# Dense products of a 62-row chunk in two column halves on TensorE, in a four-layer graph network

## The chip, the cores and the metric

The kernel runs on one core of one Trainium2 chip. A core has five engines with their own instruction queues: TensorE (PE in the profile, its weight loads are PEld), VectorE (DVE), ScalarE (ACT), GpSimd (POOL) and SyncE (SP), which here only issues DMAs. ScalarE and GpSimd issue DMAs too, from the same queue as their arithmetic. SBUF holds the working data in up to 128 partitions, PSUM takes the results of TensorE. The metric is the device time of the core in microseconds.

## The reference, cut to what matters

There are 2,708 nodes with 512 features each and a dense 0/1 adjacency matrix `adj`. Each of four layers normalizes `x`, applies a ReLU, and adds the layer's output to `x`:

```python
# layer 0
out = (a.T @ h) @ weight;  out = out * clip(in_degree, 1)**-0.5;  x = x + relu(out)
# layer 1: each node's first 64 neighbours
x = x + leaky_relu(h @ W_line.T + b_line) + leaky_relu(mean_nb(h) @ W_nb.T + b_nb)
# layer 2: attention, 8 heads of 64
Wh = einsum('nd,hdo->hno', h, W);  x = x + elu(softmax(mask(leaky_relu(f1 + f2))) @ Wh)
# layer 3
combined = concat([h @ W_self + b_self, (mask @ h / deg) @ W_nb + b_nb])
x = x + relu(combined @ W_comb + b_comb)
```

Every layer thus has dense products of the 2,708 x 512 matrix `h` with 512 x 512 weights: one in layer 0, two in layer 1, one in layer 2, and two in layer 3 (there the kernel multiplies `W_comb` into the other two weights at the start, so that `self` and `nb` are one product each). Layers 0, 1 and 3 then aggregate over `adj`, layer 2 attends over it.

## The kernel before, in words

The nodes are cut into `NC` = 22 chunks of `R` = 126 rows; the last chunk, number 21, has `last_rows` = 62. The dense stage of a layer goes chunk by chunk: load `x` (`load_x`, line 277), normalize (`norm`, line 186), transpose four 128-column slices on TensorE and apply the ReLU on ScalarE (`relu_T`, line 208, giving `hT`), then multiply. `product` (line 182) is one dense product: four fp32 matmuls of a 126-column left side with 512 columns of weights, accumulated in one PSUM tile of 128 x 512.

What is aggregated is kept in SBUF as two fp32r numbers per value, a rounded one and the rest (`halves`, line 258): ScalarE copies the PSUM tile with rounding, VectorE subtracts the copy from the PSUM tile. An aggregation then runs one matmul with the rounded and one with the rest (`matmuls`, line 364). The last chunk has a form of its own, the tile `tail`. Its `x` was loaded twice, to partitions 0 to 61 and, from `TAIL` = 64, to partitions 64 to 125 (line 282), and so its product stands twice in PSUM, once in each half of the partitions. `tail` holds the rounded numbers in the lower half and the rests in the upper, and the aggregation takes both in a single matmul. In layer 2 the chunk is loaded once, and the product has 62 rows.

The places of the six products:

- `product0` (line 443), layer 0: dense stage and first aggregation step by step in turn, in one order of stages with lags (`staged`, line 625). Chunk 21 is the last product, and aggregation steps follow at once.
- `product1` (line 714), layer 1: `nb` and then `line` for each chunk. The first goes into `halves`; of the second, VectorE adds the bias (line 722) and applies the leaky ReLU (line 723), GpSimd adds it to `x` (line 726), and ScalarE's queue stores `x1` (line 727). `move` (line 95) cuts a store of 62 rows in two, 48 and 14 rows. The aggregation starts after chunk 21; VectorE makes its weights `kt` (`weight1`, line 739) in three buffers.
- `product2` (line 919), layer 2: ScalarE copies the result to `wh`, which is stored and multiplied with the attention vectors. Attention steps follow.
- `nb3` and `self3` (lines 1253 and 1258), layer 3: as in layer 1, with a bias add on VectorE (line 1263) and a store of `s3`. VectorE makes the aggregation's weights `kt3` (`weight3`, line 1294) after the check of the inputs (`judge`, line 1299) has begun.

Within an engine, work runs in the order of its queue, which the framework's scheduler lays down when the program is built. Order between engines is by semaphores. `load_weight` (line 170) fills one of two weight buffers, so a weight is loaded when the one before the last is no longer read: the weights `w2s` of layer 2 (line 737) take the buffer of layer 1's `wn`. Two reductions `wmax` over `w2s` (line 772) are VectorE work, and the scheduler has put them among the first `kt` of layer 1's aggregation. PSUM tiles come in turn from one pool of eight banks.

Of the kernel before, what the change touches and what calls it, by code (L numbers as in the profile page):

```python
# [8 lines left out]
F32 = mybir.dt.float32  # L9
# [6 lines left out]
ALU = mybir.AluOpType  # L16
# [6 lines left out]
R = 126  # L23

TAIL = 64
# [4 lines left out]
SLOPE1 = 0.01  # L30
# [14 lines left out]
def fast_layers(  # L45
# [36 lines left out]
    nc = tc.nc  # L82
    N, D = x_in.shape
    H, _, O = w2.shape
    NC = -(-N // R)
    NF = D // P
    O1 = O + 1

    last_rows = N - (NC - 1) * R
    assert last_rows <= TAIL and TAIL + last_rows <= R  # L90

    def rows(c):
        return min(R, N - c * R)

    def move(engine, dst, src):

        if dst.shape[0] == last_rows:
            cut = last_rows // 16 * 16
            engine.dma_start(dst[:cut], src[:cut])
            return engine.dma_start(dst[cut:], src[cut:])  # L100
        return engine.dma_start(dst, src)
# [68 lines left out]
    def load_weight(pool, src, name, tag=None, k=NF):  # L170
        w = pool.tile([P, k, src.shape[1]], F32, name=name, tag=tag or name)
        for i in range(k):
            nc.sync.dma_start(w[:, i], src[i * P : (i + 1) * P, :])
        return w

    def load_row(pool, src, name, tag=None):

        t = pool.tile([P, D], F32, name=name, tag=tag or name)
        nc.sync.dma_start(t, bass.AP(tensor=src.tensor, offset=src.offset, ap=[[0, P], [1, D]]))
        return t  # L180

    def product(po, lhsT, w, n):
        for f in range(NF):
            nc.tensor.matmul(po[:n], lhsT[:, f, :n], w[:, f, :], start=(f == 0), stop=(f == NF - 1))  # L184

    def norm(xc, n, scalar=False):

        st = small.tile([P, nc.vector.BN_STATS_DIM], F32, name="ln_st")
        nc.vector.bn_stats(st[:n], xc[:n])  # L189
        mv = small.tile([P, nc.vector.BN_AGGR_DIM], F32, name="ln_mv")  # L190
        nc.vector.bn_aggr(mv[:n], st[:n])  # L191
        rs = small.tile([P, 1], F32, name="ln_rs")
        nc.scalar.activation(rs[:n], mv[:n, 1:2], AF.Sqrt, bias=eps[:n], scale=1.0)  # L193
        nc.vector.reciprocal(rs[:n], rs[:n])
        hn = common.tile([P, D], F32, name="hn", tag="t", bufs=3)
        if scalar:
            shift = small.tile([P, 1], F32, name="ln_shift")
            nc.vector.tensor_scalar(
                shift[:n], mv[:n, 0:1], rs[:n], -1.0, op0=ALU.mult, op1=ALU.mult
            )  # L200
            nc.scalar.activation(hn[:n], xc[:n], AF.Relu, bias=shift[:n], scale=rs[:n])
            return hn
        nc.vector.tensor_scalar(
            hn[:n], xc[:n], mv[:n, 0:1], rs[:n], op0=ALU.subtract, op1=ALU.mult
        )
        return hn
# [30 lines left out]
    def dense(src, product_of, twice=True, more=(), scalar=False, rows_of=natural):  # L237

        kept = {}

        def size(c):
            return R if twice else rows(c)

        def load(c):
            kept[c] = load_x(src, c, twice=twice, rows_of=rows_of)

        def normalize(c):
            kept[c] = kept[c], norm(kept[c], size(c), scalar)

        def transpose(c):  # L250
            kept[c] = kept[c][0], relu_T(kept[c][1], size(c))

        def multiply(c):
            product_of(c, *kept.pop(c), size(c))

        return (0, load), (1, normalize), (2, transpose), (3, multiply), *more

    def halves(ring, po, c):

        if c < NC - 1:  # L260
            t = ring.tile([R, 2, D], F32R, name="halves")
        else:
            t = ring.tile([R, 1, D], F32R, name="tail", bufs=1)
        nc.scalar.copy(t[:, 0, :], po[:R])
        if c < NC - 1:
            nc.vector.tensor_tensor(t[:, 1, :], po[:R], t[:, 0, :].bitcast(F32), ALU.subtract)
        else:
            second = t[TAIL : TAIL + last_rows, 0, :]
            nc.vector.tensor_tensor(
                second, po[TAIL : TAIL + last_rows], second.bitcast(F32), ALU.subtract  # L270
            )
        return t


    loads = {}
# [135 lines left out]
    x1 = dram.tile([N, D], F32, name="x1")  # L411
    x2 = dram.tile([N, D], F32, name="x2")
    x3 = dram.tile([N, D], F32, name="x3")
    s3 = dram.tile([N, D], F32, name="s3")
    rT = dram.tile([H, NC * R], F32, name="rT")

    with ExitStack() as ring_ctx:
# [3 lines left out]
        stages1 = dense(  # L421
            x1,
            lambda *args: product1(*args),
            more=[
                (3, lambda c: save_last(c)),
# [6 lines left out]
        w0s = load_weight(weights, w0, "w0s", tag="w")  # L432
# [9 lines left out]

        def product0(c, xc, hT, n):
            po = ps.tile([P, D], F32, name="h0_ps", tag="ps")
            product(po, hT, w0s, n)
            h0[c] = halves(ring, po, c)

        with tc.tile_pool(name="l0", bufs=2) as wk:
# [173 lines left out]
            def first_dense(lag, fn):  # L622
# [3 lines left out]
                len(units),  # L626
                (0, load0),
                *[first_dense(lag, fn) for lag, fn in dense(x_in, product0, rows_of=paired)],
                (4, fenced(count0)),
                (5, fenced(sign0)),  # L630
# [12 lines left out]
        bl = load_row(wk, b_line1, "bl")  # L643
        bn = load_row(wk, b_nb1, "bn")
        wn, wl = l1_weights
# [68 lines left out]
        def product1(c, xc, hT, size):  # L714
            n = rows(c)
            pn = ps.tile([P, D], F32, name="nb_ps", tag="ps")
            product(pn, hT, wn, size)
            h1[c] = halves(ring, pn, c)
            po = ps.tile([P, D], F32, name="line_ps", tag="ps")
            product(po, hT, wl, size)  # L720
            y = common.tile([P, D], F32, name="y", tag="t", bufs=3)
            nc.vector.tensor_tensor(y[:n], po[:n], bl[:n], ALU.add)
            nc.vector.scalar_tensor_tensor(
                y[:n], y[:n], SLOPE1, y[:n], op0=ALU.mult, op1=ALU.max
            )
            nc.gpsimd.tensor_tensor(xc[:n], xc[:n], y[:n], ALU.add)
            move(nc.scalar, x1[c * R : c * R + n, :], xc[:n])

        def save_last(c):
            if c < len(groups[-1]):  # L730
# [4 lines left out]
        w2s = weights.tile([P, NF, H, O], F32, name="w2s", tag="w")  # L735
# [33 lines left out]
        def before1(c):  # L769
# [7 lines left out]
        stages2 = dense(  # L777
            x2,
            lambda *args: product2(*args),
            False,  # L780
            [(3, lambda c: save_last2(c)), (4, lambda c: sums2(c)), (6, lambda c: rows2(c))],
# [51 lines left out]
    row, weight, wh, whs, acc, sides, made, scaled = {}, {}, {}, {}, {}, {}, [], []  # L833
# [84 lines left out]

    def product2(c, xc, hT, n):
        po = ps.tile([P, D], F32, name="wh_ps", tag="ps")  # L920
        product(po, hT, w2s.rearrange("p f h o -> p f (h o)"), n)
        wh = pp.tile([R, D], F32, name="wh", bufs=3)
        nc.scalar.copy(wh[:n], po[:n])
        move(nc.sync, whd[c * R : c * R + n, :], wh[:n])
        for i in range(2):
            t = products[c, i] = pp.tile([R, H, O], F32, name="wh_a", bufs=4)
            eng = nc.gpsimd if i else nc.vector
            ins = eng.tensor_tensor(
                t[:n].rearrange("p h o -> p (h o)"), wh[:n], ar[i][:n], ALU.mult
            )  # L930
            if i == 0:
                firsts[c] = ins.ins
            else:
                nc.gpsimd.tensor_tensor(
                    t[:n, :, : O // 2], t[:n, :, : O // 2], t[:n, :, O // 2 :], ALU.add
                )
# [59 lines left out]
    kept3, l3_weights = {}, []  # L996
# [52 lines left out]
    def normalize3(c):  # L1049
        kept3[c] = kept3[c], norm(kept3[c], R)  # L1050
# [193 lines left out]
    with ExitStack() as stack:  # L1244
        ring = stack.enter_context(tc.tile_pool(name="ring3", bufs=NC - 1, reuse_waits="tile"))
        b3 = e3.tile([P, D], F32, name="b3", bufs=1)
# [4 lines left out]
        wself, wnb = l3_weights  # L1251

        def nb3(c):
            pn = ps.tile([P, D], F32, name="nb3_ps", tag="ps")
            product(pn, kept3[c][1], wnb, R)
            h3[c] = halves(ring, pn, c)

        def self3(c):
            n = rows(c)
            po = ps.tile([P, D], F32, name="self_ps", tag="ps")  # L1260
            product(po, kept3.pop(c)[1], wself, R)
            y = common.tile([P, D], F32, name="y", tag="t", bufs=3)
            ins = nc.vector.tensor_tensor(y[:n], po[:n], b3[:n], ALU.add)
            move(nc.scalar, s3[c * R : c * R + n, :], y[:n])
            return ins.ins

        def do(fn, c):
# [8 lines left out]
        for c in range(NC):  # L1276
            nb3(c)
            if c:
                do(transpose3, c + 1)
            do(turn3, c + 3)  # L1280
            do(normalize3, c + 2)
            do(save3, c + 2)
            do(elu3, c + 3)
            do(load3, c + 5)
            final = self3(c)
            if c == 0:
                transpose3(1)
# [691 lines left out]
```

## Time and profile before

| | |
|---|---|
| device time, median of 3 runs | 1822.22 us (1820.46 to 1822.46) |
| profiled execution, own time | 1820.7 us |
| its span, first to last instruction | 1818.8 us |
| mean granted TensorE clock | 0.996 |
| busy: TensorE, VectorE, ScalarE, GpSimd | 1781.6, 1307.9, 798.0, 245.3 us |
| last chunk's product in layer 0 | starts 162.46 us |
| last chunk's products in layer 1 | start 534.39 (record) us, aggregation from 541.40 us |
| last chunk's product in layer 2 | starts 850.11 us |
| last chunk's products in layer 3 | start 1581.47 us, aggregation from 1589.73 us |

The profile is one execution on the chip. Times inside it count from the start of its span. A group of instructions has a line of the kernel, an engine, an operation and shapes; the busy time of a group counts overlapping instructions once, while the mean is that of a single one, so a busy time below count times mean says that instructions overlapped. An fp32 matmul appears as two records. An arrow in brackets names what ended the idle time before an instruction. "The chain" is the work followed back from the last instruction, at each step to what released it.

### The profile page before, as it was taken

To read this page: it belongs to the slowest core of one execution; us is meant where nothing else is said; L and a number is where in the kernel's file an instruction comes from. 1 tells how busy PE (TensorE), PEld (TensorE's weight loads), DVE (VectorE), ACT (ScalarE), POOL (GpSimd) and SP (SyncE) were. 2 spreads that over 40 slices of the span, in tenths; PEclk is the share of its full clock that TensorE was granted. 3 is DMA by queue.
4 is the path that set the end of the run, shared out by engine and by line. 5 is a ranking of instruction groups with operands and counts; after the bars stand their busy time and mean duration, and the time that the engine had idled before them with its cause. 6 is when DMAs were issued, how large, how long until landed. Compare 5 with 4: busy or idle time off the path is not lost.

```text
span 1818.8 us, 30698 instructions
## 1 busy us (share of the span) xinstructions
PE 1781.6 (98%) x11884; PEld 1036.1 (57%) x11884; DVE 1307.9 (72%) x1836; ACT 798.0 (44%) x1542; POOL 245.3 (13%) x241
## 2 busy tenths in 40 slices
PE   9899999999999999999999999999999999999998
PEld 4456777654447887644444344444444454488776
DVE  4942998955546655888999999999998777533334
ACT  2642777722110000156887767767744566400000
POOL 0101333301121111266000000000001222100000
PEclk9999999999999999999999999999999999999999
DMA  7632666635461211343221121122022444313221
GB/s 248 193 114 67 204 208 196 204 76 121 117 149 55 67 54 46 97 147 104 73 61 26 42 62 43 27 61 57 13 65 56 134 131 139 94 38 102 78 69 45
DMA packets 165554, 176.63 MB, mean 97 GB/s; under 512 B 94830, under 2 KB 115792, under 8 KB 164516
## 3 DMA queue, kind: packets, MB, share of 16 engines
q1 hardware_dynamic: 143170, 131.47, 26.2%
q10 hardware_dynamic: 18484, 33.28, 5.4%
q0 software_dynamic: 3744, 9.82, 1.6%
q8 instruction: 96, 1.57, 0.4%
q14 instruction: 60, 0.49, 0.1%
HBM read 111.35 MB, written 55.15 MB: 92 GB/s over the span
## 4 chain that ended last, share of the span: by engine, by line
PE 80%; DVE 9%; issue 4%; DMA 4%; ACT 1%; POOL 1%; SPq 0%; DVEq 0%; ACTq 0%; POOLq 0%
PE acc L368 31%; PE av L1069 19%; PE nb_ps L184 7%; PE sums L1069 6%; PE self_ps L184 4%; PE wh_ps L184 3%; DVE t L886 3%; PE line_ps L184 3%; DVE cum L494 2%; PE h_ps L184 2%; PE hT_ps L212 2%; PE fused_ps L312 2%; DMA x<-x 1%; DMA ai<-in_adj 1%; DVE two L506 1%
## 5 line engine op out<-in xcount | busy, mean ns | idle before, releaser
L886 DVE SCALAR_TENSOR_TENSOR t<-rb,ec,vT 126x2708 f32<-126x2708 f32 (+2 forms) x220 | 532.2, 2472 | 17.6 <-PE sums L1069 9.7
L368 PE MATMUL acc<-halves,kt 126*126 126x512 f32 x1848 | 435.9, 395 | 3.9 <-DVE kt L741 2.3
L1069 PE MATMUL av<-t,whs 126*32 126x451 f32 (+3 forms) x4576 | 436.2, 515 | 0.6 <-DVE ln_mv L191 0.6
L368 PEld LDWEIGHTS acc<-halves,kt 126*126 126x126 f32 x1848 | 342.6, 186 | 93.7 <-DVE kt L741 6.9
L1069 PEld LDWEIGHTS av<-t,whs 126*32 126x32 f32 (+1 forms) x4576 | 158.7, 110 | 207.8 <-issue 188.0
L368 PE MATMUL acc<-halves,ar 126*126 126x512 f32 x924 | 232.7, 405 | 2.1 <-DVE deg L502 1.1
L904 ACT ACTIVATE b<-t,eb 126x2708 bf16<-126x2708 f32 (+1 forms) x78 | 199.1, 2552 | 25.4 <-DVE t L886 25.1
L368 PEld LDWEIGHTS acc<-halves,ar 126*126 126x126 f32 x924 | 169.1, 186 | 52.7 <-issue 7.7
L193 ACT ACTIVATE ln_rs<-ln_mv,eps 126x1 f32<-126x1 f32 x88 | 25.6, 293 | 339.5 <-DVE ln_mv L191 336.5
L741 DVE SCALAR_TENSOR_TENSOR kt<-lastr,index,vT 126x504 fp32r<-126x504 int16 (+3 forms) x154 | 110.6, 729 | 81.0 <-PE acc L368 80.7
L1296 DVE CAST kt<-vT 126x504 fp32r<-126x504 uint8 (+3 forms) x154 | 56.0, 366 | 138.2 <-PE acc L368 138.2
L1069 PE MATMUL sums<-t,whs 126*32 126x338 f32 (+5 forms) x1568 | 139.6, 449 | 2.4 <-ACT out L1110 2.4
L874 ACT ACTIVATE whs<-wh,ef 126x64 f32<-126x64 f32 x220 | 76.8, 349 | 130.6 <-PE sums L1069 66.1
L1036 POOL TENSOR_SCALAR z<-y 126x512 f32<-126x512 f32 x22 | 44.0, 2000 | 662.2 <-DVE y L1029 653.4
L494 DVE TENSOR_TENSOR_SCAN cum<-ai,deg 126x504 int16<-126x504 int32 (+2 forms) x110 | 128.6, 1182 | 0.5 <-DMA ai<-in_adj 0.5
L522 ACT ACTIVATE cum<-cum,limit 126x504 int16<-126x504 int16 (+3 forms) x132 | 88.2, 668 | 58.4 <-DVE deg L502 57.3
L1069 PEld LDWEIGHTS sums<-t,whs 126*32 126x32 f32 (+1 forms) x1568 | 54.9, 109 | 70.0 <-issue 43.7
L189 DVE BATCH_NORM_STATS2 ln_st<-x 126x6 f32<-126x512 f32 x88 | 60.4, 686 | 43.1 <-DMA x<-x 29.1
L184 PE MATMUL h_ps<-w0s,hT 128*126 128x512 f32 x176 | 79.7, 596 | 6.0 <-ACT hT L214 4.7
L184 PE MATMUL nb_ps<-wfn,hT 128*126 128x512 f32 x176 | 81.7, 608 | 2.0 <-ACT hT L214 2.0
L184 PE MATMUL wh_ps<-w2s,hT 128*126 128x512 f32 (+1 forms) x176 | 79.4, 593 | 0.0
L184 PE MATMUL nb_ps<-wn,hT 128*126 128x512 f32 x176 | 79.2, 592 | 0.0
(182 smaller groups left out, 1869.8 us busy)
## 6 DMA issues: line engine op xcount, KB each, us to landing
x<-x SPq DMA_DIRECT2D x105, 252.0 KB
x<-x ACTq DMA_DIRECT2D x84, 252.0 KB
ai<-in_adj SPq DMA_DIRECT2D x84, 249.0 KB
x<-in_x SPq DMA_DIRECT2D x42, 252.0 KB
rb<-rT SPq DMA_DIRECT2D x7, 1332.8 KB
wh<-whd SPq DMA_DIRECT2D x70, 94.5 KB
packed<-two POOLq DMA_DIRECT2D x44, 124.5 KB, 4.3
whd<-wh SPq DMA_DIRECT2D x21, 252.0 KB
```

The lines of the kernel that those rows point to most:

```text
L184: nc.tensor.matmul(po[:n], lhsT[:, f, :n], w[:, f, :], start=(f == 0), stop=(f == NF - 1))
L189: nc.vector.bn_stats(st[:n], xc[:n])
L368: nc.tensor.matmul(acc[:R], weight[:, k * R : (k + 1) * R], parts[:, i, :], start=(m == 0 and i == 0), stop=(m == NC - 1),)
L494: nc.vector.tensor_tensor_scan(cum[:n, :gw], ai[:n, :gw], ai[:n, :gw], 0.0 if g == 0 else deg[:n, m : m + 1], op0=ALU.add, op1=ALU.max,)
L522: nc.scalar.activation(cum[:n, :gw], cum[:n, :gw], AF.Sign, bias=limit[:n], scale=-1.0, accum_out=signs[:n, m, g : g + 1],)
L741: nc.vector.scalar_tensor_tensor(by_chunk(kt, cs), lastr[:, cs[0] * R : (cs[-1] + 1) * R].rearrange("p (c r) -> p c r", r=R), index[:R, m ...
L874: ins = nc.scalar.activation(t[:q, :O], wh.pop((u, m))[:q], AF.Copy, scale=by)
L886: ins = nc.vector.scalar_tensor_tensor(t[:q, : hi - lo], row[h][:q, lo:hi], ec[:q, m, h : h + 1], vT[g][:q, k, lo:hi], op0=ALU.max, op1=AL ...
L904: nc.scalar.activation(b[:q, : hi - lo], weight[s][:q, : hi - lo], AF.Sigmoid, bias=eb[:q, m, h : h + 1], scale=STEEP,)
L1036: nc.gpsimd.tensor_scalar(z, y, 0.0, None, op0=ALU.min)
L1069: nc.tensor.matmul(p[j * S : (j + 1) * S, : b - a], lhsT, rhs[:, part * size + a : part * size + b], start=(s % NC == 0), stop=(s % NC == ...
L1296: nc.vector.tensor_copy(by_chunk(kt, cs), pattern(m, cs))
```

## The change

`product_of_last` multiplies the last chunk in two halves of the columns. One matmul puts columns 0 to 255 into PSUM partitions 0 to 61, the other columns 256 to 511 into partitions 64 to 125, so each has a left side of 62 columns and a right side of 256. The array is then addressed as two tiles of 128 x 64, one for each half of the PSUM partitions. `any_product` takes this form for chunk 21 and the old one for all others, at all six places.

What reads the result follows its two corners. `halves` clears `tail` on GpSimd, makes three copies on ScalarE and two subtractions on VectorE, of 62 x 256 each, in place of one copy of 126 x 512 and one subtraction of 62 x 512. In layers 1 and 3 the bias add, the leaky ReLU and GpSimd's add are done for each corner, and each store becomes four DMAs of half rows in place of two of whole rows. In layer 2 the copy to `wh` is made in two parts. The loads of `x` to both halves of the partitions stay.

```diff
+    HALF = D // 2
+    corners = [
+        (slice(0, last_rows), slice(0, HALF)),
+        (slice(TAIL, TAIL + last_rows), slice(HALF, D)),
+    ]
+    def product_of_last(po, lhsT, w):
+        for f in range(NF):
+            for at_rows, at_cols in corners:
+                nc.tensor.matmul(
+                    po[at_rows, at_cols], lhsT[:, f, :last_rows], w[:, f, at_cols],
+                    start=(f == 0), stop=(f == NF - 1),
+                )
+    def any_product(c, po, lhsT, w, n):
+        if c == NC - 1:
+            product_of_last(po, lhsT, w)
+        else:
+            product(po, lhsT, w, n)
...
-        nc.scalar.copy(t[:, 0, :], po[:R])
         if c < NC - 1:
+            nc.scalar.copy(t[:, 0, :], po[:R])
             nc.vector.tensor_tensor(t[:, 1, :], po[:R], t[:, 0, :].bitcast(F32), ALU.subtract)
-        else:
-            second = t[TAIL : TAIL + last_rows, 0, :]
-            nc.vector.tensor_tensor(
-                second, po[TAIL : TAIL + last_rows], second.bitcast(F32), ALU.subtract
-            )
-        return t
+            return t
+        nc.gpsimd.memset(t.bitcast(F32), 0.0)
+        (low, first), (high, other) = corners
+        t = t[:, 0]
+        nc.scalar.copy(t[low, first], po[low, first])
+        nc.scalar.copy(t[low, other], po[high, other])
+        nc.scalar.copy(t[high, other], po[high, other])
+        nc.vector.tensor_tensor(
+            t[high, first], po[low, first], t[low, first].bitcast(F32), ALU.subtract
+        )
+        nc.vector.tensor_tensor(
+            t[high, other], po[high, other], t[high, other].bitcast(F32), ALU.subtract
+        )
+        return t.rearrange("p (i d) -> p i d", i=1)
...
-            product(pn, hT, wn, size)
+            any_product(c, pn, hT, wn, size)
             h1[c] = halves(ring, pn, c)
             po = ps.tile([P, D], F32, name="line_ps", tag="ps")
-            product(po, hT, wl, size)
+            any_product(c, po, hT, wl, size)
             y = common.tile([P, D], F32, name="y", tag="t", bufs=3)
-            nc.vector.tensor_tensor(y[:n], po[:n], bl[:n], ALU.add)
-            nc.vector.scalar_tensor_tensor(
-                y[:n], y[:n], SLOPE1, y[:n], op0=ALU.mult, op1=ALU.max
-            )
-            nc.gpsimd.tensor_tensor(xc[:n], xc[:n], y[:n], ALU.add)
-            move(nc.scalar, x1[c * R : c * R + n, :], xc[:n])
+            for own in corners if c == NC - 1 else [(slice(0, n), slice(0, D))]:
+                nc.vector.tensor_tensor(y[own], po[own], bl[own], ALU.add)
+                nc.vector.scalar_tensor_tensor(
+                    y[own], y[own], SLOPE1, y[own], op0=ALU.mult, op1=ALU.max
+                )
+                nc.gpsimd.tensor_tensor(xc[own], xc[own], y[own], ALU.add)
+                move(nc.scalar, x1[c * R : c * R + n, own[1]], xc[own])
...
-        nc.scalar.copy(wh[:n], po[:n])
+        if c == NC - 1:
+            for own in corners:
+                nc.scalar.copy(wh[:n, own[1]], po[own])
+        else:
+            nc.scalar.copy(wh[:n], po[:n])
...
-            ins = nc.vector.tensor_tensor(y[:n], po[:n], b3[:n], ALU.add)
-            move(nc.scalar, s3[c * R : c * R + n, :], y[:n])
+            for own in corners if c == NC - 1 else [(slice(0, n), slice(0, D))]:
+                ins = nc.vector.tensor_tensor(y[own], po[own], b3[own], ALU.add)
+                move(nc.scalar, s3[c * R : c * R + n, own[1]], y[own])
```

`product0`, `product2`, `nb3` and `self3` call `any_product` in the same way.

More of the change, by code (lines that the diff above doesn't have):

```diff
@@ L184, in product @@
             nc.tensor.matmul(po[:n], lhsT[:, f, :n], w[:, f, :], start=(f == 0), stop=(f == NF - 1))
+    HALF = D // 2
[7 more added lines that the diff above has]
+                nc.tensor.matmul(
+                    po[at_rows, at_cols],
+                    lhsT[:, f, :last_rows],
+                    w[:, f, at_cols],
+                    start=(f == 0),
+                    stop=(f == NF - 1),
+                )
[4 more added lines that the diff above has]
+            product(po, lhsT, w, n)
     def norm(xc, n, scalar=False):
@@ L444, in product0 @@
             po = ps.tile([P, D], F32, name="h0_ps", tag="ps")
-            product(po, hT, w0s, n)
+            any_product(c, po, hT, w0s, n)
             h0[c] = halves(ring, po, c)
@@ L920, in product2 @@
         po = ps.tile([P, D], F32, name="wh_ps", tag="ps")
-        product(po, hT, w2s.rearrange("p f h o -> p f (h o)"), n)
+        any_product(c, po, hT, w2s.rearrange("p f h o -> p f (h o)"), n)
         wh = pp.tile([R, D], F32, name="wh", bufs=3)
-        nc.scalar.copy(wh[:n], po[:n])
+        if c == NC - 1:
[3 more added lines that the diff above has]
+            nc.scalar.copy(wh[:n], po[:n])
         move(nc.sync, whd[c * R : c * R + n, :], wh[:n])
@@ L1254, in nb3 @@
             pn = ps.tile([P, D], F32, name="nb3_ps", tag="ps")
-            product(pn, kept3[c][1], wnb, R)
+            any_product(c, pn, kept3[c][1], wnb, R)
             h3[c] = halves(ring, pn, c)
@@ L1260, in self3 @@
             po = ps.tile([P, D], F32, name="self_ps", tag="ps")
-            product(po, kept3.pop(c)[1], wself, R)
+            any_product(c, po, kept3.pop(c)[1], wself, R)
             y = common.tile([P, D], F32, name="y", tag="t", bufs=3)
-            ins = nc.vector.tensor_tensor(y[:n], po[:n], b3[:n], ALU.add)
-            move(nc.scalar, s3[c * R : c * R + n, :], y[:n])
+            for own in corners if c == NC - 1 else [(slice(0, n), slice(0, D))]:
+                ins = nc.vector.tensor_tensor(y[own], po[own], b3[own], ALU.add)
+                move(nc.scalar, s3[c * R : c * R + n, own[1]], y[own])
             return ins.ins
```

## The prediction

> **What bounds the kernel now.** I read the page first: TensorE is busy 98% of the span, and every slice of it is an 8 or a 9.
>
> ```profile
> span 1818.8 us, 30698 instructions
> PE 1781.6 (98%) x11884; PEld 1036.1 (57%) x11884; DVE 1307.9 (72%) x1836; ACT 798.0 (44%) x1542; POOL 245.3 (13%) x241
> PE  9899999999999999999999999999999999999998
> PE 80%; DVE 9%; issue 4%; DMA 4%; ACT 1%; POOL 1%; SPq 0%; DVEq 0%; ACTq 0%; POOLq 0%
> ```
>
> The chain that ended last is TensorE for 80% of the span, so a microsecond taken from TensorE is worth up to a microsecond, wherever TensorE is not about to wait for something else. So I went to the six places where the last chunk is multiplied. In the groups split by shape, its 62 rows cost what 126 rows cost (columns: line, engine, operation, out<-in, shape, count | busy us, mean ns of one | idle before):
>
> ```profile
> L184 PE MATMUL wh_ps<-w2s,hT 128*126 128x512 f32 x168 | 75.8, 593 | 0.0
> L184 PE MATMUL wh_ps<-w2s,hT 128*62 128x512 f32 x8 | 3.6, 598 | 0.0
> ```
>
> Eight matmul records make one product (four slices of the weights, two records for each fp32 matmul), 3.6/8 = 0.45 us of busy time apiece. The chain in order of time (start, length, what) gives one product as 3.43 to 3.45 us, and also shows the nearest thing to the new form, the attention products, which put four 32-column tiles side by side:
>
> ```profile
> 1584.90 3.45 PE self_ps L184 x8
> 865.94 1.30 PE av L1069 x16
> 867.83 1.17 PE av L1069 x16
> 1058.83 4.56 PE av L1069 x48
> ```
>
> 48 records in 4.56 us are 95 ns apart, though each takes 543 ns: four tiles do run at once. The first such group after a full-width matmul takes 1.30 instead of 1.17 us: a switch of the array costs about 0.13.
>
> Last, the timeline around the two places where other engines come close behind TensorE:
>
> ```profile
> 541.40 11.37 PE L368 MATMUL acc<-halves,kt 126*126 126x512 f32 x48
> 543.55 1.45 DVE L741 SCALAR_TENSOR_TENSOR kt<-lastr,index,vT 126x504 fp32r<-126x504 int16 x1 [0.52 <-PE acc L368]
> 547.18 2.29 DVE L772 TENSOR_REDUCE wmax<-w2s 128x1 f32<-128x2048 f32 x1 [1.04 <-DMA w2s<-in_L_gnn_W]
> 552.23 2.04 DVE L741 SCALAR_TENSOR_TENSOR kt<-lastr,index,vT 126x504 fp32r<-126x504 int16 x3
> 553.02 3.26 PE L368 MATMUL acc<-halves,kt 126*126 126x512 f32 x13 [0.25 <-DVE kt L741]
> ...
> 1588.37 0.68 DVE L1263 TENSOR_TENSOR y<-self_ps,b 62x512 f32<-62x512 f32 x1 [2.12 <-PE self_ps L184]
> 1589.73 6.50 PE L368 MATMUL acc<-halves,kt 126*126 126x512 f32 x27 [1.39 <-DVE kt L1296]
> ```
>
> After layer 1's last product the aggregation starts at 541.40, and its seventh step waits 0.25 us for a `kt` that stood in VectorE's queue behind two reductions `wmax`, the first of which waited for a weight load. After layer 3's last product TensorE stands for 1.39 us until bias add, one reduction and `kt` are through VectorE.
>
> **What the Trainium skill says.** "TensorEngine Tiling (Array Packing)", Theoretical Speedup: a left side of at most 64 columns allows up to 2x; Key Properties: tiles load weights and multiply in parallel, but a change of mode drains the array. The 95 ns agree with the parallel tiles (four of 32 columns; two of 64 are not in this trace), the 0.13 us with the drain. "SBUF — State Buffer", SBUF: two separate sides: VectorE with two SBUF inputs and a GpSimd operation that reads SBUF exclude each other for a whole instruction. The trace agrees: the `kt` at 543.55 took 1.45 us instead of 0.73, and GpSimd's add `x` of line 726 ran from 543.17 to 544.46.
>
> **The change part by part.**
>
> Products. Each becomes 16 records of 256 columns instead of 8 of 512. A 512-column record starts 0.43 us after the one before (3.44/8), so one of 256 takes 0.215; two tiles at once make 8 slots, 1.72 us, about 1.75 with small gaps, plus 0.15 once per place for the switch. Weight loads: 134 ns for 62 columns (the mean of the eight loads of the short `wh_ps`), two in a slot of 215 ns; the 32-column loads, 110 ns, are hidden at one per 95 ns, so I cost these at nothing; uncovered they would be 2.1 us per product.
>
> Layer 0 (162.46 to 165.90, among aggregation steps): 3.44 - 1.90 = 1.55 us. The halves of this chunk are read only at 173.9, and the three copies (a 512-column copy takes 0.58 us, a 126-column one 0.25; I estimate 0.36 for 256) and two subtractions need less than 2 us: hidden. TensorE stays full until 303.9. From there to 393 it has gaps and VectorE, GpSimd and DMAs carry the chain, but that stretch begins on the chain at TensorE's end of a group (303.88, then `nrm`, `y`, `x`, the `packed` stores), so it moves along. I take 1.55; bounds 0 and 1.7.
>
> Layer 1 (two products, 534.39 to 541.26): TensorE is done 6.87 - 3.65 = 3.2 us sooner, and aggregation could start at 538.2. But what feeds it does not move. VectorE's adds for the last chunk wait for copies behind ScalarE's store of chunk 20, which GpSimd releases at 539.82; with two subtractions and four half adds they end near 543, as before. Then `kt` 3 comes at about 544.4, the weight load still lands at 547.06, the first `wmax` ends at 549.4, the second at 552.4. In the changed program's order one more `kt` stands ahead of the first `wmax`; so the `kt` behind both serves step 7 instead of step 6. It comes at 553.1 in both; TensorE is then one step of eight matmuls ahead (1.9 us) less some 0.2. I take 1.7; bounds 0 and 3.2. The other 1.5 us go into TensorE's waits for `kt` between 543 and 553.
>
> Layer 2 (850.11 to 853.69, 3.58): 1.65 us saved; its scaled copy and sums come 1.0 to 1.6 us sooner as well. The next weights `t` are four deep; `t` 3 was ready 0.6 us before use, and moves by 1.0 when TensorE moves by 1.65, so it is just in time. I take 1.65; bounds 0.6 and 1.75.
>
> Layer 3 (1581.47 to 1588.35): 3.2 us sooner. Behind it: three copies end 1.1 us and the subtractions 1.5 us after the first product, before the second ends at 1.75, so the bias add is not held. The add in two halves costs about 0.1 more than 0.68. I take 3.1; bounds 2.2 and 3.3.
>
> Around these: three `memset`s of the tail (0.52 us each, the row of line 281). GpSimd's first waits for the start's weight stores, as the next one did at 44.4, and its next work is at 52.6. The second falls into its 24 us idle before 391.6, the third between operations that end at 1412.1 and begin at 1420.7. Two more DMAs each for the stores of `x1` and `s3` (0.3 to 0.45 us to issue, ScalarE idle behind them). On SyncE a load of `x` moves ahead of two weight loads whose first use is after 1411. Nothing.
>
> Sum: 1.55 + 1.7 + 1.65 + 3.1 = 8.0 us. Against the profiled execution's own 1820.7: 1812.7. The median of the runs shown is 1822.2, which would give 1814.2; the four executions lie between, and I say 1813.5. What measurement of this kernel can tell from no change is about 0.2%, 3.6 us.
>
> **The rivals.**
>
> Given back later: the tiles work, but slack elsewhere swallows part. Layer 0's share is lost if the loads of `adj` (up to 230 GB/s between 180 and 350 us) set the pace from 303 to 393 rather than the group's end; layer 1's, if `wmax` or its load comes 2 us later than I place it. Then 1.65 + 3.1 remain, or a little less: 1816 to 1818.5. Against it: the chain runs through TensorE before 303.9, with no idle from 166 to 300.
>
> The change doesn't do what it says: two 64-column tiles take turns. Then 16 x 0.22 + 0.15 = 3.65 us against 3.44, 0.2 more for each of six products, and 0.3 in the edges: 1822.5 to 1823.5. Against it: four 32-column tiles do not take turns.
>
> Slower: the tiles take turns and their weight loads cannot run under the other tile's matmul. A load of 134 ns then stands open 16 times: 2.1 us, the product 5.8 instead of 3.44, six times 2.3 = 14 us, less layer 1's cover: 1834. It decides from 0.6 us more per product (3.6/6), that is 25 ns open per load once the tiles take turns. Against it: the hidden 110 ns loads of the attention.
>
> **How the numbers follow.** As computed 0.70 (own range 1811 to 1816.5); given back 0.14 (about half of it still beyond 0.2%); taking turns 0.06; slower by weight loads or by something the trace of before does not show 0.10. Faster 0.70 + 0.07 = 0.77; same 0.07 + 0.06 = 0.13; slower 0.10. The range 1810.3 to 1820.0 holds the first case with its bounds and the second.
>
> **What would show it.** In the changed profile a 62-column product should be 16 records of about 1.75 us in all, two starting together. The four places should show the aggregation starting about 3.2 us sooner after layer 1's dense stage and then about 1.5 us of TensorE waiting for `kt` L741; the wait before layer 3's first aggregation should stay near 1.4 to 1.5 us. Wrong would be: starts 0.2 us apart with no overlap, TensorE idle in layer 0 growing after 303, or more than 3 us of waiting behind `wmax`.

## The result and the profile after

The changed kernel takes 1814.3 us (median of 6 executions, 1812.12 to 1816.08), the kernel before 1821.93 beside it (1818.29 to 1825.81). The ratio is 0.9955 with a 95% interval of 0.9945 to 0.9965, or 8.2 us less (6.4 to 10.0). The prediction was 1813.5 in a range of 1810.3 to 1820.0. The profiled execution took 1814.06 us.

The page's first part and its chain, in the columns of the page shown before:

```profile
span 1812.3 us, 30823 instructions
PE 1775.4 (98%) x11932; PEld 1042.1 (57%) x11932; DVE 1310.9 (72%) x1842; ACT 801.3 (44%) x1549; POOL 247.4 (14%) x245
PE 83%; DVE 8%; DMA 3%; issue 3%; ACT 1%; POOL 1%; SPq 0%; DVEq 0%; ACTq 0%; POOLq 0%
```

The kernel is as much TensorE's as before: 6.2 us less busy time, 6.5 us less span. Six products with 16 records for 8 account for the 48 additional instructions on TensorE.

The group of the short product (shape, count, busy us, mean ns), and the chain in order of time (start us, length us, what) at layers 0, 1 and 2:

```profile
L197 PE MATMUL wh_ps<-w2s,hT 128*62 128x256 f32 x16 | 1.9, 386 | 0.0
```

```profile
163.37 1.88 PE h_ps L197 x16
...
536.06 1.88 PE nb_ps L197 x16
537.93 1.73 PE line_ps L197 x16
539.66 0.36 PE last_ps L708 x2
...
848.10 1.88 PE wh_ps L197 x16
849.98 1.30 PE av L1107 x16
```

Sixteen records, each of half the columns, fit into 1.9 us where eight took 3.6: so both tiles run at a time, and no weight load stands open. A product alone takes 1.88, the second of two in a row 1.73: the 0.15 between them fits the switch of the array that the prediction put at 0.15. In layer 2 the attention follows as before with its 1.30.

The timeline (start us, length us, engine, line, operation; in brackets the idle time before and what ended it) behind layer 1's and layer 3's last products:

```profile
539.77 22.48 PE L401 MATMUL acc<-halves,kt 126*126 126x512 f32 x95
547.12 2.29 DVE L806 TENSOR_REDUCE wmax<-w2s 128x1 f32<-128x2048 f32 x1 [0.55 <-DMA w2s<-in_L_gnn_W]
...
1579.60 0.36 ACT L296 CAST tail<-nb_ps 62x256 fp32r<-62x256 f32 x1 [4.67 <-PE nb_ps L197]
1581.20 0.43 DVE L302 TENSOR_TENSOR tail<-nb_ps,tail 62x256 fp32r<-62x256 f32 x1
1581.66 0.88 DVE L1302 TENSOR_TENSOR y<-self_ps,b 62x256 f32<-62x256 f32 x2
1583.33 8.85 PE L401 MATMUL acc<-halves,kt 126*126 126x512 f32 x37 [2.05 <-DVE kt L1335]
```

In layer 3 the wait before the aggregation has grown from 1.39 to 2.05 us. In layer 1 the aggregation runs on from 539.77 almost without a wait.

Stage by stage on TensorE, the two profiled executions compare thus (us, from the starts of the records; "step 12" is the 13th group of eight matmuls of layer 1's aggregation):

| stage | before | after | difference |
|---|---|---|---|
| first record to layer 0's last product | 158.67 | 159.84 | +1.17 |
| to layer 1's last `nb` | 372.10 | 372.68 | +0.58 |
| to step 12 of layer 1's aggregation | 29.84 | 26.34 | -3.50 |
| to layer 2's last product | 285.88 | 285.70 | -0.18 |
| to layer 3's last `nb` | 731.19 | 729.58 | -1.61 |
| to layer 3's aggregation | 8.42 | 5.73 | -2.69 |
| to the last record | 221.51 | 221.47 | -0.04 |

The sum is -6.27. The surprise is the second row, where layer 0 should have given 1.55, and the first row, which holds nothing of the change. So the question for the experiments is whether each layer gives what its products save, and what the two rows hide.

### The profile page after: what moved, and what is told of

Its sections match the earlier page's. It is cut to its first block, busy times and chain, and to the rows that moved or that the text cites. A ratio compares the mean times of both kernels' runs of the same rounds, so it can differ in the third digit from the quotient of the medians.

```text
span 1812.3 us, 30823 instructions
## 1 busy us (share of the span) xinstructions
PE 1775.4 (98%) x11932; PEld 1042.1 (57%) x11932; DVE 1310.9 (72%) x1842; ACT 801.3 (44%) x1549; POOL 247.4 (14%) x245
## 4 chain that ended last, share of the span: by engine, by line
PE 83%; DVE 8%; DMA 3%; issue 3%; ACT 1%; POOL 1%; SPq 0%; DVEq 0%; ACTq 0%; POOLq 0%
PE acc L401 32%; PE av L1107 19%; PE nb_ps L184 8%; PE sums L1107 6%; PE self_ps L184 4%; PE line_ps L184 4%; PE wh_ps L184 3%; DVE t L920 3%; PE h_ps L184 2%; DVE cum L527 2%; PE hT_ps L237 2%; PE fused_ps L345 2%; DMA ai<-in_adj 1%; DMA packed<-two 1%; DVE two L539 1%
## 5 line engine op out<-in xcount | busy, mean ns | idle before, releaser
L184 PE MATMUL nb_ps<-wfn,hT 128*126 128x512 f32 x168 | 77.3, 604 | 2.0 <-ACT hT L239 2.0
L521 ACT ACTIVATE ar<-ai 126x504 fp32r<-126x504 int32 (+2 forms) x132 | 74.9, 568 | 2.9 <-DMA ai<-in_adj 2.9
```

Of the source, the lines that this page charges most:

```text
L521: nc.scalar.activation(ar[:, :gw], ai[:, :gw], AF.Square, accum_out=squares[:R, m, g : g + 1])
```

## Experiments

**Theory**: each layer's saving stands on its own as predicted, and what blurs it are stretches at half TensorE clock that come by chance. **Rival**: layer 0's saving is lost in the stretch behind its TensorE-bound groups, whose pace other engines and DMAs set, so that layer 0 gives nothing. Four kernels use the new form in one layer alone, and the kernels before and after run unchanged as a measure of the scatter.

No edit (`before_again`, `after_again`):

> The kernel before, unchanged, for a second profile. Theory 1 (the half-clock stretches of 3.4 us at 77 and 395 us in the changed kernel's profile come by chance from execution to execution): such stretches move about here too, and the starts of the last chunk's products differ from the first profile's (162.5, 534.4, 850.1, 1581.5 us) by up to 2 us in the first two places; ratio 1.000. Theory 2 (the change brings them): none here before 1000 us, as in the first profile.

> The changed kernel, unchanged, for a second profile and more timing. Theory 1 (half-clock stretches by chance, and layers 0 and 1 share one bound, the kt that stands behind both wmax at about 553 us): without a half-clock stretch before 540 us, the aggregation of layer 1 starts near 538.3 and TensorE then waits 1 to 1.6 us in all for kt L775 before 554; with one, it starts near 540 and waits for nothing; the product of layer 2 starts at 848 in both. Theory 2 (the change brings the stretches): the same two stretches near 77 and 395 us again. Both: 6.5 to 8.5 us below the kernel before.

Measured: ratio 1.0 (0.9991 to 1.0008), and 0.9966 (0.9954 to 0.9979), which is 6.2 us less, just under what was expected. Between the two traces of before, the starts of the last products moved by 3 to 6 us, and not by the 2 expected.

New form in layer N alone (`only_l0` to `only_l3`; `halves` and the edges of layers 1, 2 and 3 follow the same condition):

```diff
-    def any_product(c, po, lhsT, w, n):
-        if c == NC - 1:
+    SPLIT = (N,)
+    def any_product(layer, c, po, lhsT, w, n):
+        if c == NC - 1 and layer in SPLIT:
```

> The new form in layer 0 alone; the other five products as before. Prediction as on record (each place pays for itself): 1.5 us faster, product of layer 1 starts 1.5 us sooner. Theory 1 (shared bound: what feeds kt at 553 us hangs on DMAs that layer 0's product does not move): the product itself is 1.88 us instead of 3.44, but TensorE waits longer for the kt behind wmax, about 1.0 to 1.7 us there instead of 0.25, and the device time falls by 0 to 0.5 us.

> The new form in layer 1 alone. Prediction as on record: 1.7 us faster, aggregation starts 3.2 us sooner and TensorE waits about 1.5 us for kt before 554 us. Theory 1 (shared bound) says the same for this run, 1.7 to 2.0 us, and that this is all that layers 0 and 1 give together.

> The new form in layer 2 alone. Prediction as on record: the product takes 1.9 us instead of 3.58, the layer-3 product starts 1.65 us sooner after it (729.6 instead of 731.2 us from the start of layer 2's last product, where no half-clock stretch falls between), 1.6 us faster. Rival (VectorE, which is full from 930 us on, absorbs it): 731.2 stays, no gain.

> The new form in layer 3 alone. Prediction as on record: from the first of the two products to the first aggregation matmul 5.3 us instead of 8.42 (3.1 us gained, wait for kt 1.4 to 1.5 us). What the changed kernel's profile says: 5.73 (2.7 us gained, wait 2.05 us, because copies, subtractions and half adds on VectorE are of 0.43 us, not 0.36). Rival (the longer pause trips the clock gate): in some executions a half-clock stretch of 3.4 us begins right behind the wait and takes 1.5 us of it back.

| kernel | ratio, 95% interval | us less | in its trace, against before |
|---|---|---|---|
| `only_l0` | 0.999 (0.998 to 0.9999) | 1.8 (0.2 to 3.6) | groups 0 to 3 of layer 0 end 1.1 to 1.45 sooner |
| `only_l1` | 0.9991 (0.9984 to 0.9997) | 1.6 (0.5 to 2.9) | step 12 is 27.66 behind the last `nb`; the five runs with the old form here: 29.33 to 29.88 |
| `only_l2` | 0.9998 (0.9989 to 1.0008) | 0.4 (-1.5 to 2.0) | layer 2's last product to layer 3's: 729.50 for 731.19 |
| `only_l3` | 0.999 (0.9981 to 0.9999) | 1.8 (0.2 to 3.5) | last `nb` to aggregation: 5.73 for 8.42 |

Together the four times make 5.6 us, with intervals too wide to tell that from the 6.2 and 8.2 of the whole change. An account in the expectations, that layers 0 and 1 share one bound (the `kt` behind both `wmax`), is out: `only_l0` reached step 12 after 29.33 us, no later than any other with the old form there.

Layer 0: in all three executions of the changed kernel (`after_third`, below, is the third) the last matmuls of groups 0 to 3 start 1.45 us sooner after the last product's start (10.87, 53.80, 96.76 and 139.73, for 12.32, 55.26, 98.21 and 141.18 to 141.21); `only_l0` lost 0.35 of it in group 3. Behind that, one kernel differs from itself: the last matmul of group 5, the last group, started 213.10 and 216.27 us after that product in two executions of before, and 212.02, 212.21 and 213.92 in three of after. The 216.27 and the 213.92 have a half-clock stretch on the way (see below), at 360.3 and 355.6 us.

Behind the groups the saving does not last in the traces. On the way to layer 1 the degrees of the nodes are stored by one DMA and loaded again by another. The chain of before, and then that of the changed kernel (start us, length us, what):

```profile
368.48 9.23 DMA degd<-deg
377.76 3.51 DMA rdeg<-degd
```

```profile
368.48 8.90 DMA degd<-deg
377.43 4.28 DMA rdeg<-degd
```

Five traces have the old form in layer 0, and eight the new, interleaved one. From the issue of this store to the first operation on the loaded degrees it took 12.24 to 13.20 us with the old form and 13.23 to 14.20 with the new. The store itself was still issued 1.07 us sooner after the last product in the mean (205.73 for 206.80). The transposes of layer 1 that wait for this chain, near 394 us, came 231.54 us after that product for 231.60: nothing is left. From the end of group 3 to these transposes TensorE stood idle for 5.13 to 7.16 us with the old form and for 7.19 to 8.76 with the new. So the traces speak for the rival, and only the time of `only_l0`, whose interval just leaves out zero, speaks against it. Which holds, and why the two DMAs took longer, stays open.

Layer 2's interval holds its 1.7 us as well as nothing, but the traces can be compared. From layer 2's last product to layer 3's it is 731.19 to 731.22 us in three executions with the old form and 729.58 and 729.61 in two with the new, all five with the same half-clock stretches on the way: 1.6 us less. The 729.50 of `only_l2` lacks the stretch near 1005 us. The other executions with the new form there have 728.15 to 728.78 in three with fewer stretches, and 731.13 and 731.17 in two with one more.

Layer 3 shows what blurs the times. In `only_l3` the aggregation's own length grew from 221.5 to 223.05 us. A window of its trace (stretch and its length, then busy us and count of PE, PEld, DVE, ACT and POOL; the granted clock is the third number from the end) that holds the end of the wait, at 1592.52:

```profile
1592.00:1596.00 4.00, 3.48 (x9) 2.74 (x10) 2.54 (x14) 0.00 (x0) 0.00 (x0) 0.64 0.71 225
```

The same place in the changed kernel's trace, wait ending at 1583.33:

```profile
1582.00:1586.00 4.00, 2.67 (x12) 2.19 (x13) 3.60 (x17) 0.00 (x0) 0.00 (x0) 1.00 0.57 187
```

The same wait of 2.05 us is followed once by a stretch at half clock and once by none. The records of the granted clock give every such stretch a length of 3.41 us, or twice that, at 0.5 of full speed (one more, at the very end where TensorE has no work left, is not counted here); in `only_l3` it cost 223.05 - 221.49 = 1.56 us. They stand in all 14 executions that were traced, of both kernels and all variants: `before_again` has them at 80.4 and 360.3 us, where the first trace of before had none ahead of 1006. They begin about 2 to 4 us behind the start of a pause of TensorE of 1.8 to 3.1 us. A pause of 2.6 to 2.9 us near 75 us drew one in 9 of the 14, a pause of 2.4 near 1004 us in 10 of 14, the new wait of 2.05 us in layer 3 in 2 of 5.

The traces also show what this chance hangs on. Within each trace, all stretches begin whole multiples of 3.413 us apart (in the first one of the changed kernel 93, 271 and 389 of them behind the first stretch). TensorE's records can be cut into windows on this grid, from 60 us on. In all 14 traces, every one of the 33 windows with at least 2.0 us of idle TensorE is followed by a stretch; of those with 1.4 to 2.0 us, 15 of 39 are; below that none is, unless it is at half clock itself. So a pause draws a stretch when enough of it falls into one window, and where the windows begin differs from execution to execution.

The Trainium skill, "TensorE: Matmul & The Clock Gate", Part 1, has a free-running activity window of about 3.4 us that decides on half or full clock, and says that results vary from run to run with its phase. The length, the grid and the chance agree; but there an idle window of about 3.4 us is needed, and here 2.0 us of idle time in a window were always enough, and pauses from 1.8 us sometimes. The clock row of the profile's page shows a 9 in every slice of the changed kernel: a slice of 45 us hides such a stretch.

With that the first two rows above are read: the changed kernel's execution had stretches at 77.2 and at 394.7 us that the one of before had not, some 1.5 us each. Two windows inside them, in the same columns:

```profile
77.30:80.50 3.20, 3.10 (x4) 1.51 (x5) 3.20 (x9) 1.04 (x4) 0.53 (x1) 0.50 0.40 121
394.70:398.00 3.30, 3.30 (x6) 1.23 (x5) 2.77 (x7) 1.64 (x4) 0.13 (x1) 0.50 0.38 104
```

The first row is explained by one of them, and most of what the second lacks (2.0 us) by the other. A stretch near 395 us stands in six of the eight traces with all six products changed and in none of the six others, three of which have no pause of more than 0.8 us there. So it is not ruled out that the change makes this one likelier.

**Does the order of the two halves matter?** In `tile_by_tile` all four slices of one half are multiplied first, then those of the other; the instructions are the same.

```diff
-        for f in range(NF):
-            for at_rows, at_cols in corners:
+        for at_rows, at_cols in corners:
+            for f in range(NF):
                 nc.tensor.matmul(
```

> The changed kernel with the two loops of the product exchanged: first all four matmuls of the lower tile, then all four of the upper one, so that the same matmuls and weight loads no longer alternate between the tiles. If two tiles run at once only when their matmuls are neighbours in the queue: 16 records 0.215 us apart, 3.4 to 3.6 us per product, ratio 0.999 to 1.002 of the kernel before. If the array finds the second tile's matmuls behind seven of the first: 1.9 us as in the changed kernel. If weight loads are what the alternation hides: more than 4 us per product.

Measured: 0.9984 (0.9973 to 0.9994), 2.9 us less than before. A single product takes 2.79 us, and the two of layer 1 4.63 instead of 3.6. None of the three expected cases came true. Its timeline in layer 3:

```profile
1580.98 2.21 PE L197 MATMUL nb_ps<-wfn,hT 128*62 128x256 f32 x13
1582.82 0.43 PE L197 MATMUL self_ps<-wfs,hT 128*62 128x256 f32 x1
1583.03 0.38 PE L197 MATMUL nb_ps<-wfn,hT 128*62 128x256 f32 x1
1583.08 0.38 PE L197 MATMUL self_ps<-wfs,hT 128*62 128x256 f32 x1
```

Records of the second product, which begins with the first tile, run beside the last ones of the first product, which are on the second tile. So the tiles overlap without regard to which product the work is from, but only between instructions that are close to each other in the queue. How close, the single product of layer 2 shows: taken in the order of the program, the second tile's first record starts 0.92 us after the first tile's first, beside the fifth of that tile's eight. Four records alone, four pairs and four alone are 12 slots of 0.216 us, 2.6 us, and the switch. Turn about, 1.88 us; grouped by tile, 2.79; one at a time would be 3.44. The interleaved loop is worth about 0.9 us for a product alone and 1.0 us for two in a row. Why the second tile starts four records ahead and not sooner is not shown.

**Layer 3's wait.** In `self_first` the last chunk multiplies `self` before `nb`, so that the bias add, and behind it `judge` and `kt`, can run under the second product:

```diff
+            if c == NC - 1:
+                final = self3(c)
             nb3(c)
...
-            final = self3(c)
+            if c < NC - 1:
+                self3(c)
+            kept3.pop(c)
```

> The changed kernel with the two products of the last chunk exchanged in layer 3: self before nb. The bias add then runs under nb, and copies and subtractions of the tail, which is read only 41 us later, stand behind the first kt. If VectorE's queue behind the last product is what the wait of 2.05 us is: it falls to 0.1 to 0.5 us, 5.73 us from the first product to the aggregation becomes 3.8 to 4.2, 1.5 to 1.9 us faster than the changed kernel, 8.5 to 10 us below the kernel before. If kt waits for something else (its buffers): nothing changes.

> The kernel self_first once more, beside the changed kernel on the same chip. Theory (TensorE's 2.05 us wait for kt before layer 3's aggregation is on the path, and nothing else moves): 2.0 to 2.2 us below the changed kernel, and up to 3.7 where the wait is followed by a half-clock stretch of TensorE. Rival (the wait is made up for later): the changed kernel's time within 0.5 us.

> The changed kernel itself, as the measure for the other three on this chip: ratio to the kernel before 0.9955 to 0.9966, as in its two earlier runs.

Measured: `self_first` 0.9939 (0.9919 to 0.9959) on one chip; on another `self_first_2` 0.994 (0.9927 to 0.9953) and, beside it, `after_third` 0.996 (0.9947 to 0.9973). The difference of those two ratios is 3.6 us, of the medians (1813.15 and 1814.93) 1.8. The timeline of `self_first`:

```profile
1581.39 1.95 PE L197 MATMUL self_ps<-wfs,hT 128*62 128x256 f32 x16
1583.16 1.90 PE L197 MATMUL nb_ps<-wfn,hT 128*62 128x256 f32 x16
1583.38 0.87 DVE L1302 TENSOR_TENSOR y<-self_ps,b 62x256 f32<-62x256 f32 x2 [1.19 <-PE self_ps L197]
1584.49 1.07 DVE L1339 CAST kt<-vT 126x504 fp32r<-126x504 uint8 x3
1585.05 8.12 PE L401 MATMUL acc<-halves,kt 126*126 126x512 f32 x34
```

The first `kt` is there before the products end, and the aggregation starts 3.66 us after the first product instead of 5.73: 2.1 us gained, with nothing given back (221.45 and 221.52 to the end). The copies and subtractions of `tail` moved behind `kt`, to 1585.60 and later, at no cost: that chunk is aggregated last. The intervals of the two ratios overlap, so the times alone do not prove the gain; they fit the trace's 2.1.

**Layer 1's waits.** The prediction laid them on the two reductions `wmax`. In `wmax_later` these are pinned behind later `kt` and spread over two groups, and `both` has `self_first`'s edit too:

```diff
-            if c == 2 * KMAX:
-                for i, op in enumerate((ALU.max, ALU.min)):
+            if c in (2 * KMAX, 3 * KMAX):
+                i = c // KMAX - 2
+                op = (ALU.max, ALU.min)[i]
+                with tc.issue_after(kts[-1]):
                     nc.vector.tensor_reduce(
```

> The changed kernel with the two wmax reductions of layer 1 spread out: each is pinned behind a later kt in VectorE's queue, and one group apart, so that no kt stands behind both. Theory (TensorE's waits for kt behind wmax take what layer 1's two products save beyond 1.7 us): TensorE's waits for the kt of line 775 between 543 and 553 shrink from 2.1 us in four to under 1, step 12 of the aggregation starts 25.3 to 25.8 us after the first short product of nb instead of 26.3 to 26.8, and the time is 0.5 to 1.5 us below the changed kernel's. Rival (the pace there is set by kt itself, 1.45 us each while GpSimd reads SBUF, whatever stands among them): step 12 stays at 26.3 to 26.8 us, and the time is the changed kernel's within 0.5 us; or the wmax, now later, hold up other kt, and step 12 comes later than 26.8.

> The changed kernel with both edits: wmax later and spread in layer 1, and self before nb for the last chunk of layer 3. If each edit gives what it gives alone (self first: layer 3's aggregation starts 3.64 us after the first short product instead of 5.73, so 2.1 us; wmax later: 0.5 to 1.5 us), the time is 2.6 to 3.6 us below the changed kernel's and 9 to 12 us below the kernel before (ratio 0.9935 to 0.995). If wmax later gives nothing, it is self_first's time.

Measured: `wmax_later` 0.9951 (0.9938 to 0.9963), median 1816.14, not told apart from `after_third`; `both` 0.9943 (0.993 to 0.9956), median 1813.79, `self_first_2`'s time. The timeline of `wmax_later`:

```profile
544.54 0.43 DVE L302 TENSOR_TENSOR tail<-nb_ps,tail 62x256 fp32r<-62x256 f32 x1
545.00 0.88 DVE L756 TENSOR_TENSOR y<-line_ps,bl 62x256 f32<-62x256 f32 x2
545.90 0.87 DVE L757 SCALAR_TENSOR_TENSOR y<-y 62x256 f32<-62x256 f32 x2
546.81 2.89 DVE L777 SCALAR_TENSOR_TENSOR kt<-lastr,index,vT 126x504 fp32r<-126x504 int16 x3
547.96 12.29 PE L401 MATMUL acc<-halves,kt 126*126 126x512 f32 x52 [0.84 <-DVE kt L777]
```

Step 12 came 27.21 and 26.35 us after the last `nb` in these two, not 25.3 to 25.8. The `kt` behind `wmax` no longer holds anything, but the wait stands earlier: the fourth `kt`, for step 3, is queued behind the last chunk's subtractions, adds and leaky ReLUs, and those behind ScalarE's copies of `tail`, whose own queue is held by the store of chunk 20, which GpSimd's add to `x` releases:

```profile
541.64 1.29 POOL L760 TENSOR_TENSOR x<-x,y 126x512 f32<-126x512 f32 x1 [3.10 <-DVE y L757]
546.45 2.04 POOL L760 TENSOR_TENSOR x<-x,y 62x256 f32<-62x256 f32 x2 [3.53 <-DMA w2s<-in_L_gnn_W]
```

```profile
542.96 0.31 ACTq L101 DMA_DIRECT2D x<-x  x1
543.31 0.37 ACT L297 CAST tail<-nb_ps 62x256 fp32r<-62x256 f32 x1 [3.43 <-POOL x L760]
```

So layer 1 has two limits in a row. Without any wait, step 12 would stand 3.79 + 12 x 1.853 = 26.03 us behind the last `nb`. The six executions with the change in layer 1, its full interleaving and its old `wmax` order, by the start of GpSimd's add for chunk 20 behind that product:

| kernel | GpSimd's add | step 12 | lost to waits |
|---|---|---|---|
| `after` | 2.54 | 26.34 | 0.31 |
| `self_first` | 2.86 | 26.68 | 0.65 |
| `after_again` | 3.15 | 26.76 | 0.73 |
| `after_third` | 3.77 | 27.21 | 1.18 |
| `only_l1` | 4.01 | 27.66 | 1.63 |
| `self_first_2` | 4.04 | 27.95 | 1.92 |

The later the side engines trail TensorE, the more is lost. With `wmax` moved it is less at the same lag: `wmax_later` had that add at 4.12 us and lost 1.18, `both` at 3.22 and lost 0.33, so the move is worth some 0.4 to 0.7 us in the traces, too little for the times to show. What makes them trail by 2.5 us in one execution and 4.0 in the next was not settled.

## Why the prediction was right, point by point

- **Products**: 1.75 + 0.15 for the switch, 3.65 for two. Measured 1.88 to 1.90, and 1.88 + 1.73 = 3.61. The 256-column slots, the two tiles at once, the hidden 62-column loads and the switch all stand in the trace; the rival "the tiles take turns" and the exposed loads are out. The prediction did not see that this hangs on the order of the instructions (`tile_by_tile`: 2.79).
- **Layer 0**, 1.55: 1.45 through the fourth group. That what follows "moves along" is not what the traces show: TensorE's idle time behind the fourth group grew from 6.1 to 8.0 us in the mean, a sign that the prediction itself had named for being wrong, and by layer 1's transposes nothing of the saving is left. Its rival "given back later" is right here as far as the traces tell, by way of the two DMAs of the degrees and not of the loads of `adj`. For the term speaks the time of `only_l0` alone (1.8, interval 0.2 to 3.6).
- **Layer 1**, 1.7: TensorE is through 7.00 - 3.79 = 3.21 us sooner, as said. The prediction let 1.5 of that go into waits; the runs lost 0.3 to 1.9, 1.07 in the mean, while those with the old form lost 0.1 to 0.6 (29.24 without waits; 29.33 to 29.88). So step 12 comes 2.5 us sooner in the mean, with 1.6 (0.5 to 2.9) measured for the layer alone. The place was half wrong. In four of the six executions the `kt` behind `wmax` does hold TensorE, but in the three where GpSimd's add comes about 3.8 us or more behind the product, the first and larger wait is for the `kt` behind the last chunk's adds, which `wmax_later` showed by taking the other away. VectorE's chain was said not to move, with the second `wmax` ending at 552.4, 18.0 us after the last `nb` starts; it ended 16.3 to 17.9 us after it. That the profiled execution has 552.25 is luck: its `nb` started 1.6 us later than before's.
- **Layer 2**, 1.65: 1.6 between traces with the same half-clock stretches. The attention starts 1.70 sooner.
- **Layer 3**, 3.1: 2.69. This term was mis-sized. "The bias add is not held" failed: the subtractions were said to end 1.5 us after the first product, but each of the two takes 0.42 to 0.43 and the third copy ends only 1.2 us behind the product, so they end at 1581.63, 2.05 us behind it and 0.35 us after the second product. The copies themselves (0.36 to 0.37) were sized right. The add in halves takes 0.88, 0.2 more than 0.68, not 0.1. Together that is 0.55 of the 0.66 by which the wait grew, and the rest is hand-over.
- **Memsets, extra stores, SyncE's order**, nothing: they were not measured by themselves, and whether one of them has a part in the longer DMAs behind layer 0 is open.
- **Sum**: 8.0 predicted; 8.2, 6.2 and 7.3 us in three comparisons. With the terms as the traces give them, 2.5 + 1.6 + 2.7 = 6.8 without layer 0, and 8.3 with its 1.45. That the sum fits is partly luck: layer 1 gave 0.8 more than its term, layer 3 gave 0.4 less, and layer 0 less too if the traces are right. The step from the profiled execution to the median was a choice between 1812.7 and 1814.2; it does not matter at this size.

## What to carry to other kernels

Where a left side has at most half the columns of the array, two column tiles brought fp32 products down from 3.44 to 1.88 us here, with their matmuls issued turn about (2.79 without). When a product gets shorter, list what VectorE and ScalarE do behind it operation by operation: on half the columns they take well over half the time (0.43 us for 256 where 512 took 0.68 or 0.69), and here that made up most of the 0.66 us by which the next wait grew, which reordering two products removed. A saving in a stage which side engines follow at their own pace can be worth less than TensorE's share in it, as in layers 0 and 1, and one profiled execution cannot say how much.

## What was not expected of the hardware

Pauses of TensorE of 1.8 to 3.1 us are followed, in some executions and not in others, by 3.41 us (or 6.83) at half clock, about 1.5 us lost each time. The stretches of one execution lie on one grid of 3.413 us, and 2.0 us of idle time inside one window of the grid always brought one. Two traces of one kernel differ by several of these stretches, and they must be counted before stages are compared: the execution of the changed kernel with one stretch took 1812.48 us, one with six (one of them double) 1819.16.

Two 64-column tiles overlap only over a short distance in the queue, four records here: 1.88 us turn about and 2.79 us grouped by tile, for the same 16 records.
